# WKV of batch elements two to four laid out as one evenly spaced sequence in a Flamingo block on one core

## The chip, the cores and the metric

The kernel runs on one core of a Trainium2 chip. The metric is the device time of one execution in microseconds, the median of three runs. In the text PE is TensorE, PEld its weight loads, DVE is VectorE, ACT is ScalarE, POOL is GpSimd, and SP is SyncE, whose queue issues the DMAs here.

## The reference, cut to what matters

Four batch elements `x[b]` of 512 tokens by 512 channels (float32), and a context of the same shape, pass through four residual stages:

```python
x = x + tanh(g_xattn[0]) * wkv(w, u, layernorm(x), ctx)           # recurrence over the tokens
x = x + tanh(g_ffn[0])   * bit_ffn(layernorm(x), w1, w2, w3)      # 1-bit weights, 512 -> 2048 -> 512
x = x + tanh(g_xattn[1]) * int8_attention(layernorm(x), ctx)      # 16 heads of 32
x = x + tanh(g_ffn[1])   * ternary_linear(layernorm(x), gamma, W) # 512 -> 512
```

The first stage, WKV, is the one that is moved. For each channel it runs along the 512 tokens with keys `k = layernorm(x)` and values `v = ctx`:

```python
no  = max(o, u + k);  A  = exp(o - no);      E  = exp(u + k - no)
y   = (A * p + E * v) / (A * q + E)
no2 = max(w + o, k);  A2 = exp(w + o - no2); E2 = exp(k - no2)
p, q, o = A2 * p + E2 * v, A2 * q + E2, no2
```

Elements do not depend on one another, so the WKV of element 3 may run at any time before its own FFN.

## The kernel before, in words

One element is 4 tiles of 128 tokens; its 512 channels are 4 chunks of 128. Elements are counted from 0 in the code; element 1 is the second one.

**The order.** The kernel has a planner of its own. Each layer of each element is a generator (a "line") that issues a few instructions and yields. `line(gen, (start, end, steps), ...)` gives it places: `steps` steps spread evenly from `start` to `end`. `run` (L1206) takes again and again the line whose next place is smallest and lets it issue one step. Place 0 to 0.99 is the first stretch: WKV of element 0, preparation of the weights, and the FFN of element 0, whose 16 steps are counted with `at_unit(n) = 0.3 + 0.67 * n / 16`, so `at_unit(3.6)` is 3.6 sixteenths into the first FFN. From place 1 on there is one "grid batch" for each whole number: in grid batch b runs the FFN of element b, beside it the attention of element b-1 (from slot 4.95 of its batch into slot 6 of the next), the output projection and the final ternary layer of an earlier element, and WKV of a later one. A grid batch has 17 slots (`SLOTS = NT * NF + 1`): 16 units of the FFN, a unit being one token tile and one block of 512 hidden channels, and one more.

**What the order binds.** `matmul` and `transpose` go through `in_turn`, which makes each TensorE instruction follow those of the steps before it; the first part of each layernorm in WKV is pinned too (`pinned=True`). The other instructions are put in order by the compiler's scheduler with the order of issue as a priority, so they may run ahead of their place when their inputs are ready and a buffer is free. Loads do: the load of the third element, whose place is `at_unit(10.8)`, about 248 us, starts at 103.6 us in the profile. Within an engine the built order is then fixed, and an instruction that waits holds up those behind it.

**WKV of one element** (`wkv_layer`): a layernorm (L191 to L207, DVE and POOL); four steps, one for each token tile, in which ACT writes the normalised rows `wk_xn` (L215), PE transposes them into a `wk_ps` bank and ACT copies them to `wk_k` (L584); then four chunks of nine steps, the ninth of one sharing its step with the first of the next. A chunk is a chain: DVE scan `wk_o` (L599), POOL difference `wk_p` (L608), four ACT Relus (L612) and two ACT Exps (L614), DVE scan `wk_q` (L629), POOL product (L630), DVE product (L632), DVE scan `wk_p` (L634), POOL sum and product (L635, L636), two DVE reciprocals (L640), POOL product and sum (L641, L642), the DVE product y (L645), four PE transposes into a `wy_ps` bank and the residual on DVE (L653). From the third element on, each chunk first loads its values `wk_v` by DMA. Every buffer of the chunk (`wk_o`, `wk_p`, `wk_q`, `wk_e`, `wk_v`) exists once. y lies in `wk_e`, so a chunk's Relus wait for the `wy_ps` transposes of the chunk before, and these stand in TensorE's fixed order.

**Its neighbours.** An FFN unit is 16 matmuls into two `ff_hp` banks, the gate (L745 on ACT, L746 and L750 on DVE), the quantisation (DVE, ACT, POOL at L685), four transposes into a `tp_ps` bank, and 8 matmuls into `ff_acc`, two units later. The attention's row maxima (L948) are on DVE, its Exps (L950) and most copies (L970) on ACT. In the first stretch all small PSUM tiles share two "m" banks, afterwards three.

In the version before, WKV of element 1 has its token tiles at units 2 to 5 of the first FFN and its chunks at units 5 to 14, 2.25 units to a chunk. WKV of elements 2 and 3 has its layernorm late in the batch before, its tiles at slots 1.8 to 5.8 of grid batch 1 or 2 and its chunks at slots 5.05 to 13.05 of the same batch, 2 slots to a chunk.

Of the kernel before, what the change touches and what calls it, by code (L numbers as in the profile page):

```python
# [30 lines left out]
def kernel(  # L31
# [518 lines left out]
    def load_batch(b):  # L550
        xb = st.tile([P, NT, D], F32, name=f"xb{b}", tag="xb")
        rows = x[b].rearrange("(t p) d -> p t d", p=P)
        if b:
            nc.sync.dma_start(out=xb, in_=rows)
        else:
            for t in range(NT):
                nc.sync.dma_start(out=xb[:, t, :], in_=rows[:, t, :])
        return xb
# [628 lines left out]
    def next_batch(b):  # L1187
        xs[b] = load_batch(b)
        yield
        yield from wkv_layer(b, xs[b])  # L1190
# [15 lines left out]
    def run(until):  # L1206
        while lines:
            now = min(lines, key=place)
            if place(now) > until:
                return  # L1210
            try:
                next(now["gen"])
                now["step"] += 1
                next_turn()
            except StopIteration:
                lines.remove(now)
# [3 lines left out]
    SLOTS = NT * NF + 1  # L1220

    def line(gen, *parts, aside=False):
        lines.append({"gen": gen, "parts": parts, "step": 0, "aside": aside})

    xs = {}
    with (
# [19 lines left out]
        def at_unit(n):  # L1246
            return 0.3 + 0.67 * n / 16.0
# [83 lines left out]
            (at_unit(0), at_unit(16), 64),  # L1331
            (at_unit(16), at_unit(16.4), 7),
        )
        line(next_batch(1), (at_unit(0.5), at_unit(0.5), 1), (at_unit(0.6), at_unit(0.6), 1), (at_unit(2.0), at_unit(5.0), 4), (at_unit(5.0), at_unit(14.0), 32))
        for b in (2, 3):
            line(
                next_batch(b),
                (b - 1.0 - 4.2 / SLOTS, b - 1.0 - 4.2 / SLOTS, 1),
                (b - 1.0 - 3.2 / SLOTS, b - 1.0 - 3.2 / SLOTS, 1),
                (b - 1.0 + 1.8 / SLOTS, b - 1.0 + 5.8 / SLOTS, 4),  # L1340
                (b - 1.0 + 5.05 / SLOTS, b - 1.0 + 13.05 / SLOTS, 32),
            )
        run(0.99)
    nc.sync.dma_start(out=gamma_b, in_=bcast(gamma))
    ps = ctx.enter_context(tc.tile_pool(name="ps", bufs=1, space=PSUM))
# [78 lines left out]
```

## Time and profile before

| | us |
|---|---|
| median of three runs (lowest, highest) | 1095.68 (1094.95, 1096.86) |
| the profiled execution, its own time | 1094.21 |
| span of the profile, first to last instruction | 1092.4 |
| first matmul of the first FFN | 100.2 |
| first matmul of the FFN in grid batch 1, 2, 3 | 328.6, 513.4, 738.4 |
| last FFN matmul; end | 931; 1092.4 |

Times in a view are microseconds from the first instruction. A line of the table by stretches gives the length of the stretch, for each engine its busy time and the number of instructions that ended there, then the TensorE clock that was granted (1.00 is full), the busy share of the DMA engines and their GB/s. A line of a group gives line, engine, operation, tiles and shape, the count, then busy time and mean nanoseconds of one, then the idle time before it and what ended that. A line of waits gives who waited for whom: total, number, longest.

### The profile page before, as it was taken

What the parts mean: (1) busy time and instruction counts of PE and PEld (TensorE: products, weight loads), DVE (VectorE), ACT (ScalarE), POOL (GpSimd) and SP (SyncE); (2) the same over time, 40 slices, a digit from 0 to 9 for tenths busy, and PEclk for the clock granted to TensorE, in tenths of its full rate; (3) what the DMA queues carried; (4) which work ended last, traced back from release to release, by engine and by line L of the source; (5) the groups of instructions that cost most, each with busy time, mean ns of one, the idle gap of its engine ahead of it and who ended that gap; (6) DMA issues with size and microseconds to landing.
All of it is one profiled execution on the core that took longest, in us unless ns stands there. A gap on an engine that the chain in (4) does not pass through costs nothing.

```text
span 1092.4 us, 17928 instructions
## 1 busy us (share of the span) xinstructions
PE 943.3 (86%) x6350; PEld 680.0 (62%) x6380; DVE 827.0 (76%) x1600; ACT 729.9 (67%) x1490; POOL 320.7 (29%) x328
## 2 busy tenths in 40 slices
PE   3879997998879888799997886999999999878975
PEld 2345564565557666677775665677776777655652
DVE  5985548757876899896769898966687866579976
ACT  5656755567545776667877576677685777877863
POOL 3831104423333254621215545412122410100000
PEclk8889999999999999999999798999999999989998
DMA  8188845464445674645576354655574563244311
GB/s 288 39 272 317 323 169 190 144 221 155 154 146 181 221 234 127 231 129 169 185 234 204 121 177 133 204 195 180 184 231 156 184 210 116 59 148 116 116 42 39
DMA packets 85674, 189.68 MB, mean 174 GB/s; under 512 B 12241, under 2 KB 36817, under 8 KB 74577
## 3 DMA queue, kind: packets, MB, share of 16 engines
q1 hardware_dynamic: 85584, 188.53, 51.7%
q8 instruction: 51, 0.84, 0.3%
q14 instruction: 39, 0.31, 0.1%
HBM read 148.65 MB, written 39.85 MB: 173 GB/s over the span
## 4 chain that ended last, share of the span: by engine, by line
PE 49%; DVE 22%; ACT 14%; POOL 5%; issue 5%; DMA 4%; SPq 1%; ACTq 0%; POOLq 0%; DVEq 0%
PE ff_hp L162 15%; PE pt_ps L165 7%; PE ff_acc L162 6%; PE o_ps L162 4%; PE v_ps L162 4%; PE s_ps L162 3%; ACT at_P L950 3%; DVE wk_q L640 3%; ACT at_PT L970 3%; DVE at_nm L948 2%; PE k_ps L162 2%; DVE wk_p L634 1%; PE qr_ps L165 1%; PE tp_ps L165 1%; ACT wk_e L612 1%
## 5 line engine op out<-in xcount | busy, mean ns | idle before, releaser
L162 PE MATMUL ff_hp<-wT,xp 128*128 128x512 f32 x1024 | 275.7, 412 | 6.6 <-DVE ff_z L746 3.7
L162 PEld LDWEIGHTS ff_hp<-wT,xp 128*128 128x128 f32 x1024 | 195.4, 196 | 54.6 <-DVE ff_z L746 5.7
L950 ACT ACTIVATE at_P<-s_ps,at_nm 128x512 f32<-128x512 f32 x256 | 175.0, 690 | 45.2 <-DVE at_nm L948 43.4
L948 DVE TENSOR_REDUCE at_nm<-s_ps 128x1 f32<-128x512 f32 x256 | 166.6, 677 | 38.4 <-PE s_ps L162 37.9
L970 ACT COPY at_PT<-pt_ps 128x512 f32<-128x512 f32 x224 | 131.2, 590 | 72.6 <-PE pt_ps L165 71.9
L685 POOL TENSOR_TENSOR ff_z<-qg_b,qg_s 128x512 f32<-128x512 bf16 x64 | 71.9, 1124 | 314.6 <-ACT qg_b L684 304.7
L165 PE MATMUL pt_ps<-ident,at_P 128*128 128x128 f32 x1024 | 155.4, 280 | 9.0 <-ACT at_PT L970 4.3
L165 PEld LDWEIGHTS pt_ps<-ident,at_P 128*128 128x128 f32 x1024 | 118.1, 142 | 47.3 <-ACT at_PT L970 10.9
L162 PE MATMUL ff_acc<-wT,hr 128*128 128x512 f32 x512 | 137.6, 409 | 5.2 <-DVE hr L697 2.6
L162 PE MATMUL s_ps<-at_kR,at_qR 128*128 128x512 f32 x256 | 103.0, 464 | 24.0 <-ACT at_P L950 17.6
L162 PEld LDWEIGHTS ff_acc<-wT,hr 128*128 128x128 f32 x512 | 92.9, 191 | 26.2 <-DVE hr L697 4.2
L162 PE MATMUL o_ps<-at_PT,at_V 128*32 128x128 f32 x2048 | 75.4, 281 | 4.7 <-ACT at_PT L970 2.8
L162 PEld LDWEIGHTS o_ps<-at_PT,at_V 128*32 128x32 f32 x2048 | 54.8, 111 | 28.6 <-issue 11.6
L746 DVE SCALAR_TENSOR_TENSOR ff_z<-ff_z,ff_hp 128x512 f32<-128x512 f32 x64 | 43.4, 679 | 37.0 <-ACT ff_z L745 36.9
L745 ACT ACTIVATE ff_z<-ff_hp,coef 128x512 f32<-128x512 f32 x64 | 44.1, 688 | 40.5 <-PE ff_hp L162 38.1
L750 DVE SCALAR_TENSOR_TENSOR ff_z<-ff_hp,coef,ff_z 128x512 f32<-128x512 f32 x64 | 47.7, 745 | 30.2 <-PE ff_hp L162 30.1
L684 ACT CAST qg_b<-qg_i 128x512 bf16<-128x512 int8 x80 | 49.3, 617 | 27.4 <-DVE qg_i L680 17.3
L162 PEld LDWEIGHTS s_ps<-at_kR,at_qR 128*128 128x128 f32 x256 | 43.3, 194 | 36.4 <-ACT at_P L950 25.2
L162 PE MATMUL v_ps<-wkvT,cT 128*128 128x512 f32 x128 | 60.5, 618 | 5.5 <-DVE wT L303 2.3
L162 PE MATMUL k_ps<-cT,wkvT 128*128 128x512 f32 x128 | 61.3, 631 | 2.3 <-ACT wk_k L584 1.0
L640 DVE RECIPROCAL wk_q<-wk_q 128x256 f32<-128x256 f32 x32 | 54.5, 1722 | 3.0 <-POOL wk_q L635 1.6
L696 ACT CAST hr<-tp_ps 128x512 fp32r<-128x512 f32 x64 | 37.6, 588 | 21.7 <-PE tp_ps L165 21.7
(180 smaller groups left out, 1669.4 us busy)
## 6 DMA issues: line engine op xcount, KB each, us to landing
wT<-wD SPq DMA_DIRECT2D x72, 1024.0 KB, 5.4
wn<-in_L_ffn_w_dram SPq DMA_DIRECT2D x18, 1024.0 KB, 6.2
at_kR<-kD SPq DMA_DIRECT2D x128, 128.0 KB, 4.0
at_qR<-qD SPq DMA_DIRECT2D x256, 64.0 KB, 2.5
wD<-wT SPq DMA_DIRECT2D x12, 1024.0 KB, 4.2
kD<-k_half SPq DMA_DIRECT2D x16, 512.0 KB, 2.8
qD<-at_half SPq DMA_DIRECT2D x32, 256.0 KB, 2.2
cn<-in_ctx_dram SPq DMA_DIRECT2D x8, 512.0 KB, 5.9
```

Of the source, the lines that this page charges most:

```text
L162: return in_turn(nc.tensor.matmul(*args, **kwargs))
L165: return in_turn(nc.tensor.transpose(*args))
L640: nc.vector.reciprocal(half, half)
L684: nc.scalar.copy(qb, qi)
L685: nc.gpsimd.tensor_tensor(grouped(src), grouped(qb), s.unsqueeze(2).to_broadcast([P, NG, GS]), ALU.mult)
L696: nc.scalar.copy(part[:, 0, :], pt)
L745: nc.scalar.activation(z, hp, AF.Tanh, scale=coef[:, 0:1])
L746: nc.vector.scalar_tensor_tensor(z, z, 1.0, hp, ALU.add, ALU.mult)
L750: nc.vector.scalar_tensor_tensor(z, hp, coef[:, 1:2], z, ALU.mult, ALU.mult)
L948: nc.vector.tensor_reduce(nm, sp, AX.X, ALU.max, negate=True)
L950: nc.scalar.activation(lanes[k, i, t], sp, AF.Exp, bias=nm, accum_out=sums[k][:, t, i : i + 1],)
L970: made[k] = nc.scalar.copy(dst, blocks(pt))
```

## The change

Only the places of three lines are altered; no instruction is added or taken away.

```diff
-        line(next_batch(1), (at_unit(0.5), at_unit(0.5), 1), (at_unit(0.6), at_unit(0.6), 1), (at_unit(2.0), at_unit(5.0), 4), (at_unit(5.0), at_unit(14.0), 32))
-        for b in (2, 3):
-            line(
-                next_batch(b),
-                (b - 1.0 - 4.2 / SLOTS, b - 1.0 - 4.2 / SLOTS, 1),
-                (b - 1.0 - 3.2 / SLOTS, b - 1.0 - 3.2 / SLOTS, 1),
-                (b - 1.0 + 1.8 / SLOTS, b - 1.0 + 5.8 / SLOTS, 4),
-                (b - 1.0 + 5.05 / SLOTS, b - 1.0 + 13.05 / SLOTS, 32),
-            )
+        line(
+            next_batch(1),
+            (at_unit(0.5), at_unit(0.5), 1),
+            (at_unit(0.6), at_unit(0.6), 1),
+            (at_unit(2.0), at_unit(3.6), 4),
+            (at_unit(3.6), at_unit(10.6), 32),
+        )
+        line(
+            next_batch(2),
+            (at_unit(8.0), at_unit(8.0), 1),
+            (at_unit(9.2), at_unit(9.2), 1),
+            (at_unit(10.9), at_unit(12.5), 4),
+            (at_unit(12.5), at_unit(16.0), 16),
+            (1.0 + 1.0 / SLOTS, 1.0 + 6.0 / SLOTS, 16),
+        )
+        line(
+            next_batch(3),
+            (1.0 + 3.0 / SLOTS, 1.0 + 3.0 / SLOTS, 1),
+            (1.0 + 4.5 / SLOTS, 1.0 + 4.5 / SLOTS, 1),
+            (1.0 + 7.0 / SLOTS, 1.0 + 10.0 / SLOTS, 4),
+            (1.0 + 10.0 / SLOTS, 2.0 + 7.0 / SLOTS, 32),
+        )
```

The entries are, in order: the load, the layernorm, the four token tiles, and the steps of the chunks, eight to a chunk. Worked out, the four chunks of each element lie here:

| element | before | after |
|---|---|---|
| 1 | units 5 to 14, 2.25 units a chunk | units 3.6 to 10.6, 1.75 units a chunk |
| 2, chunks 0 and 1 | batch 1, slots 5.05 to 9.05, 2 slots a chunk | units 12.5 to 16 of the first FFN, 1.75 units a chunk |
| 2, chunks 2 and 3 | batch 1, slots 9.05 to 13.05 | batch 1, slots 1 to 6, 2.5 slots a chunk |
| 3, chunks 0 and 1 | batch 2, slots 5.05 to 9.05 | batch 1, slots 10 to 17, 3.5 slots a chunk |
| 3, chunks 2 and 3 | batch 2, slots 9.05 to 13.05 | batch 2, slots 0 to 7, 3.5 slots a chunk |

The token tiles of element 2 move from batch 1, slots 1.8 to 5.8, to units 10.9 to 12.5 of the first FFN; those of element 3 from batch 2, slots 1.8 to 5.8, to batch 1, slots 7 to 10.

## The prediction

> **What bounds the kernel now.** First the page's busy times and slices.
>
> ```profile
> PE 943.3 (86%) x6350; PEld 680.0 (62%) x6380; DVE 827.0 (76%) x1600; ACT 729.9 (67%) x1490; POOL 320.7 (29%) x328
> ...
> PE   3879997998879888799997886999999999878975
> ...
> DVE  5985548757876899896769898966687866579976
> ...
> PEclk8889999999999999999999798999999999989998
> ```
>
> PE is the busiest engine, but its slices fall to 7 or 8 in two stretches, about 330 to 490 us and 570 to 690 us, just where DVE's rise to 8 and 9. A share over the span hides that, so next comes the table by stretches. I cut it at the starts of the FFN units, read off the timeline (the first `ff_hp` matmul of units 0, 5, 12 and 15 of the first FFN; slots 0, 5 and 13 of each grid batch).
>
> ```profile
> core 0: us, PE busy (x) PEld busy (x) DVE busy (x) ACT busy (x) POOL busy (x), PEclk, DMA share, GB/s
> 100.20:162.00 61.80, 57.14 (x275) 37.37 (x274) 33.47 (x66) 38.77 (x64) 7.46 (x8) 1.00 0.69 247
> 162.00:264.10 102.10, 87.24 (x390) 56.71 (x386) 72.45 (x101) 60.11 (x96) 36.20 (x36) 0.98 0.48 175
> 264.10:305.70 41.60, 37.30 (x177) 24.24 (x176) 33.18 (x67) 26.52 (x43) 13.37 (x14) 1.00 0.43 159
> 305.70:328.60 22.90, 18.32 (x78) 12.15 (x78) 15.41 (x39) 8.73 (x14) 8.91 (x11) 0.93 0.60 178
> 328.60:365.60 37.00, 34.51 (x167) 27.10 (x167) 24.72 (x48) 20.13 (x36) 9.81 (x11) 0.95 0.60 207
> 365.60:469.20 103.60, 88.03 (x590) 67.78 (x591) 96.64 (x152) 72.59 (x153) 51.80 (x51) 0.95 0.57 185
> 469.20:513.40 44.20, 41.43 (x336) 32.45 (x334) 36.42 (x88) 33.25 (x76) 9.65 (x10) 1.00 0.50 158
> 513.40:567.10 53.70, 52.48 (x423) 41.60 (x425) 35.21 (x81) 40.20 (x88) 10.57 (x11) 1.00 0.63 214
> 567.10:694.50 127.40, 102.28 (x683) 77.17 (x687) 114.17 (x206) 86.49 (x172) 67.39 (x64) 0.91 0.50 161
> 694.50:738.40 43.90, 41.77 (x334) 32.40 (x333) 32.12 (x73) 32.20 (x74) 8.00 (x8) 1.00 0.61 208
> 738.40:790.00 51.60, 50.87 (x411) 40.25 (x413) 34.75 (x80) 37.44 (x83) 10.57 (x11) 1.00 0.59 187
> 790.00:886.10 96.10, 91.88 (x667) 70.91 (x672) 75.95 (x178) 67.41 (x146) 29.27 (x29) 0.98 0.56 181
> ```
>
> Rows 567.1 and 790.0 are slots 5 to 12 of batches 2 and 3: the same FFN slots, the same stages of attention and ternary layer of the element before, one with the fourth element's WKV and one with none. They take 127.4 and 96.1 us. With WKV, DVE is busy 114.2 of 127.4 (90%), PE 80%, at a clock of 0.91; without it PE is busy 96% of the time. In batch 1 (365.6) DVE stands at 93%. So beside WKV the grid batches are bound by DVE and the chains through it, elsewhere by PE. In the first FFN DVE is at 71 to 80% and PE at 85 to 90%: less tight, not free. The waits of PE in 567.1 to 694.5 say what stands in the way: late ACT and DVE work of the attention's end and the ternary layer, which lie in the same slots.
>
> ```profile
> PE qr_ps L165 <- ACT tf_xn L231: 8.6, 1, 8.6
> ...
> PE tp_ps L165 <- DVE at_y L1036: 2.7, 1, 2.7
> ```
>
> The groups price a chunk:
>
> ```profile
> L640 DVE RECIPROCAL wk_q<-wk_q 128x256 f32<-128x256 f32 x32 | 54.5, 1722 | 3.0 <-POOL wk_q L635 1.6 <-POOL wk_p L628 1.5
> ...
> L634 DVE TENSOR_TENSOR_SCAN wk_p<-wk_e 128x512 f32<-128x512 f32 x16 | 29.4, 1838 | 2.8 <-POOL wk_e L630 2.8
> ```
>
> **The change part by part.** It moves work and removes none. Per chunk DVE takes, by the groups' means, 1.41 (L599) + 1.34 (L629) + 1.01 (L632) + 1.84 (L634) + 2 x 1.72 (L640) + 0.97 (L645) + 0.74 (L653) = 10.8 us; ACT 4 x 0.72 + 2 x 1.07 = 5.0; POOL 9.1; PE four transposes, 0.6 us end to end in the timeline. An element's token tiles take PE 4 x 0.6 = 2.4 us and ACT 4 x (0.82 + 0.59) = 5.6; a layernorm DVE 3.8.
>
> *Batch 2.* Slots 5 to 12 lose the fourth element's chunks but for the last part of one (slots 5 to 7 of 3.5 to 7: 10.8 x 2 / 3.5 = 6.2 us of DVE). The base is batch 3's 96.1; there DVE has 20 us free, so I charge half of the 6.2: 99.1 instead of 127.4, or -28.3 (bounds -25 with all of it, -31 with none). Slots 0 to 4 lose the token tiles (PE -2.4) and gain 5 / 3.5 = 1.4 chunks: DVE 35.2 + 15.4 = 50.6 of 53.7, 94%, where 92% was the limit above: 55.0, +1.3, beside PE's -2.4 + 0.8. I take +1 (-2 to +5). Batch 2: **-27**.
>
> *Batch 1* keeps four chunks and one set of tiles, spread from 8 slots to all 17. Slots 0 to 4, light so far (7.4 us each), take 1.6 chunks: DVE 24.7 + 17.3 = 42.0, at 92% 45.7 instead of 37.0; 1.2 of the 2.4 us of PE tiles may come back: +7.5. Slots 5 to 12 lose four chunks and gain 0.4 + 0.86 of one and the fourth element's layernorm: DVE 96.6 - 43.2 + 13.6 + 3.8 = 70.8, no bound any more; PE 88.0 + 2.4 - 1.6 = 88.8, at batch 3's 96% 92.8 instead of 103.6: -10.8. Slots 13 to 16 gain 1.14 chunks and lose that layernorm: 36.4 + 12.3 - 3.8 = 44.9, at 92% 48.8 instead of 44.2: +4.6. Batch 1: **+1** (-8 if the new bursts fit into DVE's gaps, +9 if little comes back in slots 5 to 12).
>
> *First FFN.* PE gets 2.4 for the tiles and 1.2 for two chunks: +3.6. The stalls: units 5 to 14 show 143.7 us with PE idle 19.2; units 0 to 4, without a chunk, 4.7 idle in 5 units, which makes 9.8 for 10.4 units. The rest, 9.4, is 2.4 us for each of four chunks. Two more cost 4.7; batch 2 shows the dear end, 31.3 / 4 = 7.8 each, so 15.7; I take the cheap end because it is this stage's own row. The four closer chunks (1.75 units instead of 2.25): 1 us each, bounds 0 and 2.4. Sum **+12** (3.6 to 29). Its cover is a chunk's own slack. In the timeline of WKV of the second element the chain from first Relu to y took 16.8, 16.2, 24.0 and 23.5 us, while the next chunk's Relus began 30.1, 29.6 and 34.3 us after the first, since they wait for these transposes:
>
> ```profile
> 227.53 0.60 PE L165 MATMUL wy_ps<-ident,wk_e 128*128 128x128 f32 x4
> ...
> 261.79 0.66 PE L165 MATMUL wy_ps<-ident,wk_e 128*128 128x128 f32 x4
> ```
>
> With 13.7 us a unit (100.2 to 305.7 for 15), 1.75 units are 24.0 us. If a chain takes longer, PE itself waits at `wy_ps`, with the FFN behind it in its fixed order.
>
> *Queues and DMAs.* SP is moved past one 1 MB load for each of two elements and four 256 KB loads of `wk_v` that come in the first FFN or earlier in batch 1. The x loads ran ahead at 103.6 and 279.4 us already; the latter waited 5.6 us for POOL's last read of the second context (L636), and that read now comes earlier. DMA is at a share of 0.43 to 0.49 there: 0, and if a `wk_v` load (4.2 us to landing) is late, up to 2 us for each of two chunks, inside the bounds above. The two pinned layernorms each find a DVE with time left; ACT in units 12 to 14 goes from 26.5 to about 31 of 41.6 (0.43 of a chunk more and a third of the tiles): 0.
>
> A rule against the change: the Trainium skill, "SBUF — State Buffer", section "SBUF: two separate sides", says that a DVE operation with two SBUF inputs and a POOL operation that reads SBUF exclude each other for the whole instruction. The rows that bear on it: the scan L634, which runs beside POOL's work, took 1210 to 2293 ns with a median of 1986; L629, the same form, 1160 to 2234 with a median of 1216. By the row's means a chunk stays at 10.8 us. By the rule's worst case every such instruction of the six chunks in the first FFN would take its longest (2.22 + 2.23 + 1.78 + 2.29 + 1.73 with 3.44 and 0.74, 14.4 us), 22 us of DVE more in all.
>
> Sum: -27 + 1 + 12 = -14 on the profiled execution's 1094.2 us (span 1092.4 and 1.8 outside it) gives 1080; the median of the runs stands 1.5 above that execution, so 1082. The first FFN's bounds lean upwards (-8, +17), for which I add 1: 1083.
>
> **The rivals.**
> *Slower: the first FFN is crowded.* Its chains exceed 24 us, as the second chunk of batch 2 did (595.8 to 628.6 and y, 33 us), PE stands at `wy_ps`, and FFN and weights queue behind. At the dear end the first FFN costs 29 and batch 1 returns nothing in exchange (+9): 29 + 9 - 27 = +11, 1107. It decides once first FFN and batch 1 together cost over 27 us, that is 4.5 for each of six chunks. For it: two shared PSUM banks, and DVE 90% in the last units. Against: 2.4 a chunk so far, and the 8 to 13 us that a finished y waited there for its transposes.
> *Even exchange.* DVE's work is the same in sum, and slots 0 to 4 and 13 to 16 of batch 1 have little room: batch 1 +9, first FFN +18, batch 2 -27: 1096.
> *More gain.* The bursts fit into gaps: first FFN +5, batch 1 -6, batch 2 -27: 1068.
> *The move does little,* because instructions run ahead of their place anyway. Against: `wk_ps` and `wy_ps` are tied to PE's order; the first `wk_xn` of the third element stood ready at 282 us and its transposes followed at 346.7. I count it with the exchange.
>
> **How the numbers follow.** Forecast, 1076 to 1092: 0.48. More gain, 1063 to 1076: 0.12. Exchange, 1093 to 1098: 0.13. Slower, 1098 to 1115: 0.27. 0.2% is 2.2 us, about what a measurement of this kernel can tell from no change. So faster 0.60, same 0.13, slower 0.27. The range 1069 to 1104 leaves out the far parts of the first and last case, about 0.2.
>
> **What would show it.** Right: slots 5 to 12 of batch 2 near 99 us with DVE under 85% and a clock near 0.98; the first FFN's 205.5 us (unit 0 to 15) 8 to 13 longer; batch 1's 184.8 within 10 of that; batch 3 unchanged. Wrong: PE waits at `wy_ps` or `wk_ps` in the first FFN, or that stretch over 25 us longer; or batch 2 losing less than 20 although the chunks have left it.

## The result and the profile after

The changed kernel takes 1100.57 us (median of 20 runs, 1092.5 to 1102.91); the one before took 1095.2 beside it (20 runs). The ratio is 1.0043, with a 95% interval of 1.0033 to 1.0054: slower by 0.4%. That lies inside the range given, on the other side from the forecast. Three of the 20 runs took 1092.5 to 1095.5 us at a mean granted clock of 0.956 to 0.959 and the other 17 took 1099.4 to 1102.9 us at 0.950 to 0.953, as the profiled one did (0.951); what sets the three apart no run shows. The profile after has a span of 1097.8 us (1092.4 before).

The page's busy times and slices of the changed kernel:

```profile
PE 944.6 (86%) x6350; PEld 681.0 (62%) x6380; DVE 828.0 (75%) x1600; ACT 728.7 (66%) x1490; POOL 323.5 (29%) x328
...
PE   3879988797968879988899999999999999878885
...
DVE  4985566867578887787898978767687866579977
...
PEclk8889998999988989989899999999999999989997
```

The work is the same, and the weak stretch of PE around 570 to 690 us is gone. A wider one has come at 190 to 570 us, where PE's slices change between 6 and 9 and the clock's between 8 and 9. The table by stretches of the changed kernel, cut at the same FFN units and slots:

```profile
core 0: us, PE busy (x) PEld busy (x) DVE busy (x) ACT busy (x) POOL busy (x), PEclk, DMA share, GB/s
100.40:168.00 67.60, 58.53 (x278) 38.19 (x277) 43.06 (x74) 43.44 (x71) 17.24 (x18) 0.97 0.64 226
168.00:273.90 105.90, 88.95 (x397) 57.75 (x394) 76.81 (x121) 64.36 (x102) 38.40 (x38) 0.97 0.53 190
273.90:325.60 51.70, 40.16 (x184) 26.25 (x184) 33.83 (x53) 29.97 (x48) 15.09 (x16) 0.96 0.27 95
325.60:351.30 25.70, 20.83 (x78) 13.48 (x78) 22.87 (x44) 8.72 (x14) 16.37 (x18) 0.82 0.60 173
351.30:395.80 44.50, 36.06 (x165) 27.36 (x164) 35.11 (x59) 25.60 (x42) 22.40 (x23) 0.92 0.54 183
395.80:496.40 100.60, 88.16 (x597) 68.98 (x600) 81.59 (x156) 64.43 (x142) 33.95 (x35) 0.93 0.56 179
496.40:547.30 50.90, 44.45 (x335) 34.56 (x334) 39.84 (x72) 36.30 (x80) 16.26 (x15) 0.93 0.49 151
547.30:605.10 57.80, 52.36 (x418) 40.58 (x417) 50.30 (x89) 45.34 (x95) 27.19 (x24) 1.00 0.59 201
605.10:700.90 95.80, 92.26 (x670) 71.36 (x677) 82.74 (x193) 67.30 (x145) 31.80 (x32) 0.98 0.55 174
700.90:743.90 43.00, 41.06 (x330) 31.90 (x329) 28.47 (x61) 32.12 (x74) 7.22 (x6) 1.00 0.73 229
```

Put together by stage, with the runs told below, in us (spans of one profile each; the first FFN is counted to the first `ff_hp` matmul of batch 1; what lies ahead of it and batch 3 with the tail change by less than 2 where they are not shown):

| kernel | first FFN | batch 1 | batch 2 | span |
|---|---|---|---|---|
| before | 228.3 | 184.8 | 225.1 | 1092.4 |
| after | 250.9 | 196.0 | 196.6 | 1097.8 |
| only the second element moved | 236.3 | 184.2 | 223.7 | 1098.7 |
| second and third moved, fourth in place | 251.8 | 172.0 | 224.9 | 1103.0 |

Batch 2 gives 28.5 back. The first FFN takes 22.6 and batch 1 takes 11.2. That is +5.3, the difference of the spans being 5.4.

In batch 2 the step is plain. Slots 5 to 12 went from 127.4 to 95.8 with DVE at 86%, PE at 96% and the clock at 0.98. The long waits of PE at `qr_ps` and `tp_ps` shown before have shrunk; these are now the longest waits of PE there (605.1 to 700.9 us):

```profile
PE ff_hp L162 <- DVE ff_z L750: 2.5, 2, 2.3
PE p_ps L162 <- DVE hr L697: 1.0, 1, 1.0
PE qr_ps L165 <- ACT at_PT L970: 0.9, 1, 0.9
```

The price of the instructions themselves hardly moved (groups of the changed kernel):

```profile
L640 DVE RECIPROCAL wk_q<-wk_q 128x256 f32<-128x256 f32 x32 | 54.9, 1729 | 4.6 <-POOL wk_q L635 3.2 <-POOL wk_p L628 1.4
L634 DVE TENSOR_TENSOR_SCAN wk_p<-wk_e 128x512 f32<-128x512 f32 x16 | 30.6, 1915 | 5.1 <-POOL wk_e L630 5.1
```

In the first FFN PE was busy 199.9 of 228.3 us before at a clock of 0.99 and is busy 208.5 of 250.9 at 0.95. So 8.6 of the 22.6 are PE's busy time, of which added tiles and transposes were to make 3.6, and 14.0 are idle. These are PE's longest waits there after the change (100 to 351 us):

```profile
PE wt_ps L165 <- DVE V L543: 5.8, 3, 4.3
PE tp_ps L165 <- ACT wT L301: 5.3, 2, 5.0
PE wt_ps L165 <- DVE hr L697: 4.8, 2, 3.9
PE wt_ps L165 <- DVE k_half L258: 3.9, 2, 2.8
PE wt_ps L165 <- ACT wi L424: 3.1, 1, 3.1
...
PE wy_ps L165 <- DVE hr L697: 1.2, 1, 1.2
```

Before the change the list began with these (100 to 329 us):

```profile
PE wt_ps L165 <- DVE k_half L258: 5.2, 2, 4.1
PE v_ps L162 <- DVE wT L303: 2.3, 2, 2.1
PE wt_ps L165 <- DVE V L543: 1.9, 3, 0.8
```

All waits at `wt_ps` and `tp_ps` together went from 15.7 to 29.1 us, which is 13.4 of the 14.0. PE does not stand at `wy_ps` waiting for a late y, as the slower rival had it (the 1.2 us is a wait for a bank). For the most part it waits for DVE and ACT to empty the two shared PSUM banks (the 3.1 us for `wi` is a wait for an input). How that comes about can be read in the timeline of the changed kernel in the fifth unit:

```profile
157.98 0.72 DVE L750 SCALAR_TENSOR_TENSOR ff_z<-ff_hp,coef,ff_z 128x512 f32<-128x512 f32 x1
158.62 1.34 DVE L632 TENSOR_TENSOR wk_q<-wk_e,wk_q 128x512 f32<-128x512 f32 x1
159.89 0.67 DVE L222 TENSOR_REDUCE qg_s<-ff_z 128x8 f32<-128x512 f32 x1
...
161.32 1.21 DVE L634 TENSOR_TENSOR_SCAN wk_p<-wk_e 128x512 f32<-128x512 f32 x1
...
162.54 1.70 DVE L640 RECIPROCAL wk_q<-wk_q 128x256 f32<-128x256 f32 x1
164.16 1.19 DVE L680 TENSOR_TENSOR qg_i<-ff_z,qg_r 128x512 int8<-128x512 f32 x1
...
165.39 0.62 ACT L684 CAST qg_b<-qg_i 128x512 bf16<-128x512 int8 x1 [3.43 <-DVE qg_i L680]
165.91 0.58 ACT L301 CAST wT<-wt_ps 128x512 fp32r<-128x512 bf16 x1
166.64 1.08 PE L165 MATMUL tp_ps<-ident,ff_z 128*128 128x128 f32 x4 [5.04 <-ACT wT L301]
```

Three WKV operations (L632, L634, L640) stand between the parts of the FFN's quantisation on DVE, which takes 7.4 us from L750 to the end of L680. ACT waits 3.43 us for it, in its fixed order the copy `wT` stands behind, and PE waits 5.04 us for that copy's bank. So much is seen. That all of the price is paid in this way is a theory, and the experiments do not bear it out as a whole.

### The profile page after: what moved, and what is told of

It is laid out like the page before. It is cut to its first block, busy times and chain, and to the rows that moved or that the text cites. A ratio compares the mean times of both kernels' runs of the same rounds, so it can differ in the third digit from the quotient of the medians.

```text
span 1097.8 us, 17930 instructions
## 1 busy us (share of the span) xinstructions
PE 944.6 (86%) x6350; PEld 681.0 (62%) x6380; DVE 828.0 (75%) x1600; ACT 728.7 (66%) x1490; POOL 323.5 (29%) x328
## 4 chain that ended last, share of the span: by engine, by line
PE 49%; DVE 20%; ACT 14%; POOL 6%; issue 6%; DMA 4%; SPq 1%; POOLq 0%; ACTq 0%; DVEq 0%
PE ff_hp L162 16%; PE pt_ps L165 7%; PE ff_acc L162 6%; PE o_ps L162 4%; PE s_ps L162 4%; PE v_ps L162 3%; ACT at_P L950 3%; DVE wk_q L640 2%; PE k_ps L162 2%; ACT at_PT L970 2%; DVE at_nm L948 2%; ACT wk_e L612 2%; DVE wk_p L634 2%; PE tp_ps L165 1%; PE qr_ps L165 1%
## 5 line engine op out<-in xcount | busy, mean ns | idle before, releaser
L162 PE MATMUL ff_hp<-wT,xp 128*128 128x512 f32 x1024 | 280.4, 417 | 9.0 <-DVE ff_z L750 6.2
L950 ACT ACTIVATE at_P<-s_ps,at_nm 128x512 f32<-128x512 f32 x256 | 174.9, 690 | 53.9 <-DVE at_nm L948 51.9
L750 DVE SCALAR_TENSOR_TENSOR ff_z<-ff_hp,coef,ff_z 128x512 f32<-128x512 f32 x64 | 47.3, 740 | 30.2 <-PE ff_hp L162 30.0
L745 ACT ACTIVATE ff_z<-ff_hp,coef 128x512 f32<-128x512 f32 x64 | 44.0, 687 | 36.3 <-PE ff_hp L162 30.5
L162 PE MATMUL v_ps<-wkvT,cT 128*128 128x512 f32 x128 | 62.7, 637 | 4.7 <-DVE wT L303 1.6
L640 DVE RECIPROCAL wk_q<-wk_q 128x256 f32<-128x256 f32 x32 | 54.9, 1729 | 4.6 <-POOL wk_q L635 3.2
```

The costliest lines, as they stand in the source:

```text
L162: return in_turn(nc.tensor.matmul(*args, **kwargs))
L640: nc.vector.reciprocal(half, half)
L745: nc.scalar.activation(z, hp, AF.Tanh, scale=coef[:, 0:1])
L750: nc.vector.scalar_tensor_tensor(z, hp, coef[:, 1:2], z, ALU.mult, ALU.mult)
L950: nc.scalar.activation(lanes[k, i, t], sp, AF.Exp, bias=nm, accum_out=sums[k][:, t, i : i + 1],)
```

## The experiments

### The parts of the change one by one

Only the second element's WKV at its new places, the two others as before:

```diff
-        line(next_batch(2), ...)   # third and fourth at their new places
-        line(next_batch(3), ...)
+        for b in (2, 3):           # as before the change
+            line(next_batch(b), ...)
```

> Only the second element's WKV gets the new places (units 3.6 to 10.6); the third and fourth stay where they were. Stages before: first FFN to the FFN of batch 1 (100.2 to 328.6) 228.4 us, batch 1 184.8, batch 2 225.0; changed kernel 250.9, 196.0, 196.6. Theory A (the added chunks and token tiles of the third element make the first FFN slow): up to unit 11 it follows the changed kernel (+5 to +9), then units 12 to 15, free of WKV, give some back; first FFN +3 to +7, batches 1 and 2 as before, 1098 to 1102. Rival (the closer spacing of the second element is what costs): first FFN +15 or more, 1110.

Measured: 1102.2 us, ratio 1.0078 (1.0054 to 1.0103). The first FFN is 236.3, so the closer places of four chunks (and of their tiles) alone cost 8.0, twice the 4 of the sum. Spacing and place moved together here: units 0 to 4, where the first chunk now begins, went from 61.8 to 67.6. The rest of the change put 14.6 more into that stage.

Second and third element at the new places, the fourth as before:

```diff
-        line(next_batch(3), ...)   # fourth at its new place
+        for b in (3,):             # as before the change
+            line(next_batch(b), ...)
```

> Second and third element as in the changed kernel, the fourth back in batch 2. Theory (batch 1 is slower because of the fourth element's tiles and two chunks in slots 7 to 17): first FFN 251, batch 1 44.5 in slots 0 to 4, then about 90 and 44, together 178, batch 2 225 again: 1110. Rival (batch 1 is slow because the third element's late chunks upset its beginning and what follows): slots 5 to 12 stay near 100 and batch 1 over 188: 1120.

Measured: 1104.81 us, 1.0095 (1.0076 to 1.0113). Batch 1 falls from 184.8 to 172.0 when two of the third's chunks and its tiles leave it and its other two move to slots 1 to 6 (-12.8). It rises to 196.0 when the fourth's tiles and two chunks come and its layernorm moves from slot 13.8 to slot 4.5 (+24.0). With these two runs the balance is +8.0 + 14.6 - 12.8 + 24.0 - 28.5 = +5.3. In slots 5 to 12 PE is busy 82.8 of 86.0 us without the fourth. From slot 5 to the batch's end PE waits for the attention's Exp (L950) to free a score bank; first the changed kernel's line, then this run's, then that of the version before (365.6 to 513.4 us):

```profile
PE s_ps L162 <- ACT at_P L950: 10.5, 7, 2.9
```

```profile
PE s_ps L162 <- ACT at_P L950: 1.9, 2, 1.1
```

```profile
PE s_ps L162 <- ACT at_P L950: 6.5, 4, 2.2
```

So 8.6 of the 24.0 us show as Exps that come late on ACT, on which WKV's Relus and Exps lie too. Against the version before, which has four chunks in these slots, it is 4.0 of the 11.2 that batch 1 lost.

### Other places for the fourth element

Second and third as before, the fourth earlier and in a row with the third:

```diff
+            (1.0 + 4.0 / SLOTS, 1.0 + 4.0 / SLOTS, 1),
+            (1.0 + 12.0 / SLOTS, 1.0 + 12.0 / SLOTS, 1),
+            (1.0 + 13.0 / SLOTS, 1.0 + 14.2 / SLOTS, 4),
+            (1.0 + 14.2 / SLOTS, 2.0 + 6.2 / SLOTS, 32),
```

> Second and third element as before; only the fourth is moved: tiles in batch 1, slots 13 to 14.2, chunks from there to batch 2, slot 6.2, 2.25 slots a chunk. Theory (batch 2's gain is real, the loss comes from the first FFN and from bursts beside an already full DVE): first FFN 228, batch 1 +5 to +10, slots 0 to 4 of batch 2 +6 to +10, slots 5 to 12 near 98: 1081 to 1092, faster than both. Rival (an even exchange wherever the chunks go): 1095.

Measured: 1109.21 us, 1.0127 (1.0098 to 1.0155). Slots 13 to 16 of batch 1 went from 44.2 to 61.0 and slots 0 to 4 of batch 2 from 53.7 to 70.5, more than batch 2's later slots gave back (127.4 to 103.5). DVE was busy only 74% of the first of these stretches. So DVE's share does not tell what a chunk costs there.

The pinned layernorm of the fourth element two slots later in the changed kernel:

```diff
-            (1.0 + 4.5 / SLOTS, 1.0 + 4.5 / SLOTS, 1),
+            (1.0 + 6.5 / SLOTS, 1.0 + 6.5 / SLOTS, 1),
```

> The changed kernel with one number altered: the fourth element's pinned layernorm at slot 6.5 of batch 1 instead of 4.5, after the third element's last chunk. Theory (its four pinned statistics, 3.2 us of DVE in the middle of that chunk, are what makes slot 5 take 18.2 us where the run with the fourth element in place has 13.6): slot 5 near 14, batch 1 191 to 193, 1095 to 1098. Rival (slot 5 is long because of the chunk itself): slot 5 stays at 17 or more, 1100.

Measured: 1101.71 us, 1.007 (1.0048 to 1.0093). Slot 5 of batch 1 fell from 18.2 to 13.6 and batch 1 from 196.0 to 192.1, so the wait at the pinned layernorm, costed at nothing, was 4.6 us in its slot. Slot 0 of batch 2 rose from 10.2 to 16.0, and nothing was won.

The fourth's chunks wider, from the start of batch 2, with layernorm and tiles at the end of batch 1:

```diff
+            (1.0 + 12.8 / SLOTS, 1.0 + 12.8 / SLOTS, 1),
+            (1.0 + 13.8 / SLOTS, 1.0 + 13.8 / SLOTS, 1),
+            (1.0 + 14.2 / SLOTS, 2.0, 4),
+            (2.0, 2.0 + 13.05 / SLOTS, 32),
```

> Second and third element as before; the fourth keeps all four chunks in batch 2 but starts at slot 0 instead of 5.05 (tiles in slots 14.2 to 17 of batch 1, chunks over slots 0 to 13.05, 3.26 slots each). Theory (slots 5 to 12 of batch 2 are dear, 7.9 us a chunk, slots 0 to 4 cheap, about 3): slots 0 to 4 +2 to +5, slots 5 to 12 12 shorter, 13 to 16 of batch 1 +2 to +5: 1087 to 1093. Rival (what leaves slots 5 to 12 costs as much elsewhere): 1095 to 1100.

Measured: 1093.21 us, 0.9991 (0.9975 to 1.0006), no difference. Batch 2 gained 5.7, batch 1 lost 3.0.

The third's four chunks from the start of batch 1, two of the fourth behind them:

```diff
+            (1.0, 1.0 + 1.2 / SLOTS, 4),
+            (1.0 + 1.2 / SLOTS, 1.0 + 9.2 / SLOTS, 32),
...
+            (1.0 + 9.4 / SLOTS, 1.0 + 10.4 / SLOTS, 4),
+            (1.0 + 10.4 / SLOTS, 1.0 + 14.4 / SLOTS, 16),
+            (2.0, 2.0 + 7.0 / SLOTS, 16),
```

> The first FFN as before; third element's tiles in slots 0 to 1.2 of batch 1 and chunks in 1.2 to 9.2, fourth element's layernorm at 9.0, tiles 9.4 to 10.4, two chunks in 10.4 to 14.4 of batch 1, the other two in slots 0 to 7 of batch 2 as in the changed kernel. Theory (batch 2's gain of 28 is real; the price lay in the first FFN and in slots 13 to 16 of batch 1; a chunk costs 4 to 6 us in slots 1 to 13 of batch 1): first FFN 228, batch 1 195 to 203, batch 2 197 to 200: 1078 to 1086. Rival (two more chunks cost batch 1 their full DVE time of 11 us each and more): batch 1 over 210, 1093 or more.

Measured: 1110.75 us, 1.0141 (1.0117 to 1.0165). Batch 1 is 218.9. Its slots 0 to 4 took 55.6 instead of 37.0, with DVE at 80% and PE at 70%.

### A lighter chunk

Each of these leaves a piece of the chunk out of the changed kernel, in elements one to three (the second to the fourth).

```diff
+                if b:
+                    half = half[:, 0:8]
                 nc.vector.reciprocal(half, half)
```

> The changed kernel with the two reciprocals of each chunk of elements two to four done on 8 columns instead of 256; the rest of the division is left out. That takes about 3.3 us of DVE from each chunk and 0 from POOL. Theory (the long DVE operations of a chunk, run as one burst, hold up the DVE work that frees the PSUM banks and feeds PE): first FFN shorter by 2 to 4 us for each of six chunks, 12 to 20 in all, batch 1 shorter by 8 to 15. Rival (POOL's part, the chain's length or the order of the steps): first FFN shorter by under 6.

Measured: 1117.4 us (one run). DVE's work in the first FFN fell by 12 us, and the stage grew from 250.9 to 265.0. A new wait stood in it (waits of this run, 100 to 366 us): DVE, no longer kept busy, waits at y for POOL.

```profile
DVE wk_e L647 <- POOL wk_e L644: 13.5, 5, 3.7
```

With that POOL work gone as well:

```diff
-            nc.gpsimd.tensor_tensor(E, E, v, ALU.mult)
-            nc.gpsimd.tensor_tensor(A, A, p[:, 0:T], ALU.mult)
-            nc.gpsimd.tensor_tensor(A, A, E, ALU.add)
+            # these three for b == 0 alone
```

> As m1 (the changed kernel with reciprocals on 8 columns for elements two to four), and also without the last three POOL operations of each of these chunks (E times v, A times p, A plus E), about 4.4 us of POOL a chunk, so that y does not wait for POOL. That part of y is left out. Theory (what lengthened m1's first FFN from 250.9 to 265.0 is DVE standing 13.5 us at the y product, with the emptying of PSUM banks queued behind it): that wait falls below 3 us and the first FFN to 238 to 250. Rival (the order built for a shorter chunk is worse by itself, or fewer DVE operations don't help): 258 or more.

Measured: 1102.3 us (one run). The wait at y is gone and the first FFN is 256.6, between the two expectations and still above 250.9.

```diff
             for i, (sign, at) in enumerate(...):
+                if b and i < 2:
+                    continue
...
+            if b:
+                yield True
+                A, E2 = A2, E
```

> The changed kernel with half of ACT's work in WKV of elements one to three: of the four rows of exponents only the last two are made (two Relus and one Exp instead of four and two), and the rest of the chunk uses these in place of the others; the output of these elements is not the reference's. DVE's and POOL's work is unchanged. ACT does about 2.5 us less for each chunk, 15 us in the first FFN. Theory that ACT's burst, with tanh L745 and the copies L684 and L301 behind it, sets the price: first FFN from 250.9 to between 236 and 243. Rival, that it is DVE's order: 246 to 254.

Measured: 1095.64 us (one run). First FFN 254.7, just above the rival's 246 to 254 and far from the theory's 243: less work on ACT did not shorten it. Batch 1 fell from 196.0 to 186.4.

```diff
+            if b:
+                yield True
+                return
             pt = bank("wy_ps")
```

> The changed kernel without the last step of each WKV chunk of elements one to three: the four PE transposes into a shared bank and the residual on DVE (L653) are left out, so the WKV of these elements is not added to x; y is still worked out. It takes the use of a shared bank, 0.6 us of PE, 0.74 us of DVE and the tie of the next chunk to PE's fixed order from each chunk. Theory, that the shared bank and the fixed order of PE set the price: first FFN from 250.9 to between 228 and 241 us. Rival, that the burst on DVE, POOL and ACT sets it wherever it falls: 243 to 253 (six times the 0.6 us of PE off, and little more).

Measured: 1089.83 us (one run). First FFN 251.1: taking away the chunk's own bank and its tie to PE's order did not shorten the stage. Batch 1 is 186.4 again, and 188.2 in the run without POOL's last operations, so its fall under less ACT work does not single ACT out. In these three runs batch 2 is 3 to 4 us longer than in the changed kernel (199.7 to 200.3 beside 196.6), so part of that gain moved on.

### Another order on DVE

A WKV operation on DVE is put behind the last quantisation issued (`behind` adds an order, and no wait, on one engine):

```diff
+        def late(ins):
+            if b and "quant" in turn:
+                behind(ins, turn["quant"])
...
+            late(nc.vector.tensor_tensor_scan(q[:, 1:], ...))
```

> The changed kernel with an order added on DVE: every WKV operation of elements one to three stands behind the int8 quantisation (L222, L676, L678, L680) that was issued last, so no scan, product or reciprocal falls between the absolute maximum and the quantised product. In the built order of the changed kernel 8 of 70 such chains are broken, by 12 WKV operations in all, in the version before 7 by 8. No work is added or removed. Theory, that the price of a chunk is paid by chains broken into: 12 operations of about 1.5 us stood in the way, so the first FFN falls from 250.9 us to between 234 and 243 and the whole to between 1083 and 1093. Rival, that the price lies in the delay of the bank copies (L258, L301, L543, L697) or in the chunk's own work, not in these chains: first FFN 246 to 256, the whole 1096 to 1106.

> The same order on DVE added to the version before, with its places. Theory: 8 operations of about 1.5 us leave the chains, the whole falls by 5 to 12 us from about 1095 to between 1083 and 1090. Rival: within 4 us of 1095, since the operations are only put elsewhere on the same engine.

> The same order on DVE added to the version with only the fourth element's chunks spread wider (slots 0 to 13.05 of batch 2), which took 1093.2 us and had 5 broken chains with 6 operations. Theory: 3 to 9 us less, 1084 to 1090. Rival: 1089 to 1097.

Measured: 1119.34 us, 1.0235 (1.0205 to 1.0265); 1110.96, 1.0155 (1.0135 to 1.0174); 1121.31, 1.0241 (1.0223 to 1.0259). All three are slower, so the theory's remedy fails. With all chains whole but one, the first FFN of the first is 261.6; with all whole, that of the second is 239.9 (228.3 without the order). The waits of the first in that stage (lines are shifted by four) show what the order costs by itself:

```profile
POOL wk_p L612 <- DVE wk_o L603: 24.1, 3, 11.4
...
PE wt_ps L165 <- DVE k_half L258: 8.8, 3, 5.2
```

The chunk's first scan, put back, holds POOL up for 24.1 us in three waits, and PE waits longer for the copy `k_half` than with the chains broken (8.8 against 3.9). What the broken chains cost by themselves these runs do not show.

The same with the bank copies (L258, L303, L543, L697) in the place of the quantisation:

> The changed kernel with another order added on DVE: every WKV operation of elements one to three stands behind the DVE copy out of a shared PSUM bank (L258, L303, L543, L697) that was issued last. Nothing else is altered. Theory, that the price of a chunk is paid by banks released late, because the copies stand behind WKV operations on DVE: the first FFN falls from 250.9 us to between 234 and 243, the whole to between 1083 and 1093. Rival, that WKV put back on DVE only comes later and holds up other copies and chains, as with the order behind the quantisation (261.6 us): first FFN 250 to 265, the whole 1098 to 1115.

Measured: 1109.38 us, 1.0131 (1.0115 to 1.0146); first FFN 253.3, with waits at `V` and `k_half` of 5.9 and 3.9 us, as without. This order did not shorten them.

### What a chunk costs in the first FFN

The changed kernel without the chunks of the first FFN, then with DVE's part of them alone, then with ACT's and POOL's:

```diff
+            if b == 1 or (b == 2 and c < 2):
+                ...        # nothing; or one part, fed from the keys
+                return
```

> The changed kernel without the chunks that lie in the first FFN (all four of element one, two of element two; their layernorms and token tiles stay; the output of these elements is not the reference's). It gives the first FFN's length with no chunk in it, which the prediction could only estimate: by 3.0 us for each chunk (2.4 of stall and 0.6 of PE) the version before has 228.3 - 12 = 216 us, and with the 2.4 us of the added tiles this kernel 218. If all six chunks of the changed kernel cost the 4.3 us of stall that its PE idle time gives, and 0.6 of PE, it is 250.9 - 29 = 222. If closer spacing and tiles carry the rest of the loss by themselves, it is 228 or more. Batch 2's slots 5 to 12 stay at 95 to 97.

> The changed kernel, in which the six chunks that lie in the first FFN have DVE's part alone: the three scans, the product, the two reciprocals, the product y, the transposes and the residual, each fed from the keys or from DVE's own results; POOL's and ACT's instructions of these chunks are left out (the output of these elements is not the reference's). Without these chunks the first FFN took 225.5 us, with them whole 250.9. Theory, that the price is paid by instructions that wait in DVE's, POOL's and ACT's fixed order for one another: DVE's part alone waits for nobody, 226 to 236. Rival, that DVE's occupation (10.8 us a chunk, standing before the FFN's own chain) sets it whoever feeds it: 240 to 251.

> The changed kernel, in which the six chunks in the first FFN have ACT's and POOL's part alone: the difference, four Relus, two Exps, five POOL products and sums, the transposes and the residual, fed from the keys; the scans, the reciprocals and the other DVE operations of these chunks are left out (the output of these elements is not the reference's). Theory of waits for one another: no DVE operation stands between, so 226 to 236. Rival, that DVE's occupation sets it: 226 to 232 as well. If ACT's and POOL's occupation set it: 240 to 251.

Measured (one run each): 1058.95, 1075.33 and 1084.1 us. The first FFN of the three, as the table by stretches of each has it:

```profile
99.40:324.90 225.50, 199.79 (x910) 130.83 (x910) 128.15 (x248) 125.25 (x204) 40.58 (x43) 0.97 0.57 199
```

```profile
99.30:332.90 233.60, 202.25 (x929) 132.19 (x929) 169.90 (x294) 120.59 (x198) 32.01 (x36) 0.98 0.54 189
```

```profile
100.70:335.80 235.10, 205.88 (x930) 134.26 (x929) 128.23 (x247) 146.53 (x234) 78.00 (x82) 0.96 0.54 187
```

The first does not hold quite what its name says. In its trace one of the third element's later chunks has run ahead into the first FFN (scans at 268, 276 and 279 us), where the changed kernel has six chunks. So five chunks are worth 250.9 - 225.5 = 25.4, or 5.1 each if they cost alike, and the stage without any would be 220.4 (an estimate from these two rows). Beside that base DVE's part of six chunks costs 13.2 and ACT's and POOL's 14.7, together 27.9 of 30.5, with the transposes and the residual counted in both. Both runs lay where the theory of mutual waits had them (226 to 236), but that range was set from 225.5, with a chunk still inside.

Units 0 to 11 need no estimate: the run without chunks has none there, and the others have the second element's four. In order: without chunks, DVE's part, ACT's and POOL's part, the changed kernel.

```profile
99.40:255.20 155.80, 142.60 (x657) 93.14 (x656) 84.61 (x164) 90.86 (x148) 17.61 (x19) 0.99 0.64 229
```

```profile
99.30:263.50 164.20, 145.56 (x672) 95.23 (x671) 118.44 (x200) 90.59 (x148) 18.17 (x19) 0.98 0.61 217
```

```profile
100.70:257.10 156.40, 142.78 (x671) 93.47 (x671) 90.48 (x168) 107.78 (x172) 47.81 (x51) 1.00 0.64 227
```

```profile
100.40:273.90 173.50, 147.48 (x671) 95.94 (x670) 119.87 (x194) 107.80 (x172) 55.64 (x55) 0.97 0.57 204
```

Four chunks cost 17.7 here, 4.4 each. DVE's part alone costs 8.4 and ACT's and POOL's 0.6, so half of the price comes only when both are there. In the rest of the stage, with the third element's two chunks, it is the other way round: 69.4 with DVE's part, 78.6 with ACT's and POOL's, 77.4 with the whole chunks, and no row without any. So for the second element's chunks DVE's part and the parts together share the price about equally. That the second half is waiting on one another fits, but it is not shown, since each run also has its own built order.

### A version that beats both

The fourth element once more in batch 2, its tiles at slots 0 to 3 and its chunks from slot 3, 2.5 slots to a chunk; the rest as before the change:

```diff
+            (1.0 + 14.0 / SLOTS, 1.0 + 14.0 / SLOTS, 1),
+            (1.0 + 15.0 / SLOTS, 1.0 + 15.0 / SLOTS, 1),
+            (2.0, 2.0 + 3.0 / SLOTS, 4),
+            (2.0 + 3.0 / SLOTS, 2.0 + 13.05 / SLOTS, 32),
```

> Elements one and two as in the version before; the fourth element's load and layernorm at slots 14 and 15 of batch 1, its tiles at slots 0 to 3 of batch 2, its chunks at slots 3 to 13.05 (2.5 slots a chunk instead of 2). The version with slots 0 to 13.05 had batch 2 at 219.4 us (225.1 before) but batch 1 at 187.8 (184.8 before), because tiles and layernorm went there. Theory: tiles and chunks out of batch 1 keep that at 184 to 186, batch 2 gains 3 to 6, the whole 1089 to 1092. Rival, that chunks cost by the place their bursts fall on: within 3 us of 1095 with batch 2 at 222 to 228.

Measured: 1088.04 us, 0.9932 (0.9916 to 0.9949), faster than both. Slots 0 to 4 and 5 to 12 of its batch 2:

```profile
508.70:567.60 58.90, 55.23 (x462) 43.13 (x463) 44.59 (x90) 49.17 (x107) 18.50 (x18) 1.00 0.60 209
567.60:682.70 115.10, 95.78 (x664) 73.33 (x668) 106.92 (x191) 76.10 (x157) 57.66 (x56) 0.94 0.52 163
```

Against 53.7 and 127.4 that is +5.2 and -12.3, with batch 1 at 186.9 (+2.1) and the first FFN unchanged at 228.3. DVE is at 93% of the second stretch, more than the 90% before, in 12 us less. Whether earlier tiles or the wider spacing brings it was not separated.

## Why the prediction was wrong, by its own steps

**Batch 2** was right: -27 expected, -28.5 measured. Slots 5 to 12 came to 95.8 (99.1 expected), slots 0 to 4 cost 4.1 (+1, bounds -2 to +5), and two misses of 3 us took each other out.

**The first FFN** was mis-sized: +12 expected, +22.6 measured, inside its bounds of 3.6 to 29. Two terms failed, and both are measured. The closer places of the second element's four chunks were given 4 and cost 8.0. The third element's two chunks, tiles and layernorm were given 8.3 (3.6 of PE and 4.7 of stall) and cost 14.6; how these divide between chunks and tiles no run shows. The two added chunks were given 3.0 each (2.4 of stall and 0.6 of PE), the price at 2.25 units, although they lie at 1.75 units themselves. At that spacing a chunk of the second element cost 4.4 in units 0 to 11, or 5.1 by the estimate over the whole stage. With the 236.3 of the run that moved it alone, this leaves (228.3 - 236.3 + 4 x 4.4) / 4 = 2.4 for a chunk before the change, or 3.1 with 5.1 (estimates), so the 3.0 is a fair reading of its own row. (Units 5 to 14 are ten units, not 10.4; that makes 2.5 of stall instead of 2.4 and decides nothing.) "I take the cheap end because it is this stage's own row" was the step that decided: the row belonged to this stage, but to another spacing and other units.

**Batch 1** was the larger miss for its size: +1 expected (-8 to +9), +11.2 measured. The working let DVE below 92% hide what came and gave slots 5 to 12 back 10.8 us. They gave back 3.0, with DVE at 81% and PE at 88%. Slots 0 to 4 cost 7.5 (7.5 expected) and slots 13 to 16 6.7 (4.6). That DVE's free share hides a chunk is the assumption that fell, here and in the two runs with more WKV in batch 1. Of what it left out the wait at the pinned layernorm is shown (4.6 in its slot, 3.9 in the batch). The late Exps of the attention are seen (4.0 us more of waiting than before), but three different cuts in the chunk took 8 to 10 us off this stage, so which engine's part delays them is not settled.

**The rivals.** The slower one named the right condition: first FFN and batch 1 together cost over 27 us, and they cost 33.8; 1100.6 lies in the interval it was given. Its mechanism was wrong: PE waits for the release of shared banks and the score banks, and hardly at `wy_ps`.

**The rule on SBUF.** The prediction weighed the Trainium skill, "SBUF — State Buffer", section "SBUF: two separate sides". The scan L634 took a mean of 2192 ns in the first FFN before and 1932 after, the product L632 737 and 1012, so the dear end of 22 us did not come. With POOL's part of these chunks left out, the scan in its place took 1352 and the product 681, while the reciprocals stayed at 1723 (1730). The other scan (L629, 1225 in the changed kernel) took 1440 in that run, which feeds it from other tiles. In sum the direction agrees with the page, at about 1 us a chunk.

**What stays open.** Spacing and place of the second element's chunks were not moved apart. Nor is it clear why a lighter chunk did not make the first FFN shorter. Leaving out a piece of the chunk, or setting an order on DVE, gave 251 to 265 us, while leaving a whole half out gave 234 and 235. Every such edit also makes the compiler build another order on all engines, and an order alone moved this stage by 2.4 to 11.6. The runs cannot separate the two.

## What to carry to other kernels

Price a moved step at its new spacing and place: here a chunk cost 2.4 to 3.1 us at 2.25 units and 4.4 to 5.1 at 1.75 and somewhat earlier, in one stage and with the same work (estimates from the rows above). A free share of the busiest engine is no cover for a chain that runs through three engines; look in the new place for the other engines' bursts, pinned instructions and shared banks, and move one part at a time. The part that pays may be small: starting one element earlier in its own batch, and wider, won 7 us, where the whole sequence lost 5.

## What was not expected of the hardware

The granted clock carried part of the loss in the first FFN. In the changed kernel's timeline PE waits 3.07 us, and its next eight matmuls take 3.76 us, where eight of the same kind take 2.11 a little later:

```profile
325.58 0.29 PE L165 MATMUL wt_ps<-identb,wi 128*128 128x128 bf16 x1 [3.07 <-ACT wi L424]
325.63 3.76 PE L162 MATMUL ff_hp<-wT,xp 128*128 128x512 f32 x8
...
333.98 2.11 PE L162 MATMUL ff_hp<-wT,xp 128*128 128x512 f32 x8
```

The granted clock is 0.50 from 325.6 to 329.0 us and 1.00 from 332.4. The Trainium skill, "TensorE: Matmul & The Clock Gate", section "Part 1: The HAM clock gate", says that the clock falls to half after an idle window of about 3.4 us. The half agrees with the row; whether that window sets it, no run here shows. Of the 8.6 us of PE's added busy time in the first FFN, 5.0 are left after the added tiles and transposes, while its clock fell from 0.99 to 0.95: part of a wait seems to be paid twice there. Over the whole span it evens out: PE's busy time went from 943.3 to 944.6, with the clock of batch 2's slots 5 to 12 up from 0.91 to 0.98.
